# The block for outlier nodes in a four-layer graph network: selection values in two half tiles, stores one by one, loads moved ahead, clears on GpSimd

## The chip, the cores and the metric

The kernel runs on one core of one Trainium2 chip. The metric is the device time of one execution in microseconds; the kernel before takes 5758.06 us (median of three runs, 5743.28 to 5765.65). The engines are named as in the profile: PE (TensorE, with PEld for its weight loads), DVE (VectorE), ACT (ScalarE), POOL (GpSimd) and SP (SyncE, which only issues DMAs).

## The reference, cut to what matters

Sixteen graphs of 1024 nodes with 64 features pass through four layers. Before each layer the features are normalised and cut at zero. Layer 0 is the costly one. Each node drops a part of its neighbours by a rule on their rank, and then, for each of 64 features, takes the quartiles over the features of the neighbours that are left:

```python
rank = jnp.cumsum(ni, axis=-1) - ni
rem = neigh & (sk > 1) & (rank % sk == sk - 1) & mask[:, :, None]
...
s = jnp.sort(vals, axis=2)
...
for tau, w in zip(TAUS, WTS):
    pos = tau * jnp.maximum(nv - 1, 0)
    lo, hi = jnp.floor(pos), jnp.ceil(pos)
    agg = agg + w * (v_lo + frac * (v_hi - v_lo))
```

A two-matrix perceptron on x + agg follows. Layer 1 sends messages through the dense adjacency matrix into a gated recurrent unit, layer 2 sends them into a tanh layer, layer 3 is an attention over the whole matrix (a softmax over 1024 x 1024 scores). Each layer adds its result to x.

## The kernel before, in words

**The idea of layer 0.** The kernel sorts each feature over all nodes of a graph once. A quartile of a node's neighbours is then a search: for how many of the first k sorted values is the node a neighbour? These counts are matrix products of the reduced adjacency matrix with 0/1 blocks (`wt`), made for 56 words of eleven sorted values each. Signs of the counts choose the word, bit operations (`places`) choose the place in it, and matrix products with tables of value differences give candidates, from which `pick` takes one by five masked copies.

**Pairs of graphs.** The graphs go in eight pairs. For each pair there are three stages.

1. *Selection* (`weights`, `select`), one graph after the other: PE counts (L1120), ACT takes the counts out of PSUM (L1128) and makes the signs (L1175), DVE finds the word (L1186 to L1197) and picks values (L1228). It searches only the windows of words in which nearly all quartiles lie. After each graph, `compact` (L1247) gathers the few nodes, up to 64 per graph, with a quartile outside these windows: a 0/1 matrix `sel` tells which node goes to which of the 64 places, their adjacency rows come by an indirect DMA, and PE counts for all 56 words (L1311, seven pieces of 56 matmuls together). ACT copies each piece into `xr` (L1315), a buffer for two pieces; SP stores it to `x_d` in DRAM (L1316); the transposed `sel` goes to `sel_d` (L1323).
2. *The extra block* (`extras`, L1326) treats the compacted nodes of both graphs, 64 of each, as one tile of 128. ACT's queue loads the words (L1331). DVE clears two tables (L1335), and SP fills them from `t_d` in eight loads of 96-byte runs (L1337). DVE makes the biases `qx` (L1343). For three quartiles ACT shifts the words (`y_x`, two buffers, L1349), PE transposes them (L1356), ACT makes signs (L1359), and DVE takes the maxima (L1363 to L1370, with `maxima`, L1024). After `places`, there is one round for each of six statistics: PE fills the candidates `cand`, one tile of four PSUM banks (L1380), DVE picks from it (L1088) and adds to `agg_x` (L1095, L1097). Last, two rounds bring the result back to the nodes: SP loads the selection matrix into `sel_t`, one buffer (L1388), PE multiplies (L1391), DVE writes flagged nodes (L1392).
3. *Layers 0 to 3* (`layers`, L1398) of the two graphs, each with pools of its own. The first loads are `h0` (L1492) and `xb` (L1495), in two parts each; the first operation is the sum at L1497, the last the one at L1609. The blocks of the transposed adjacency matrix come from `a_d` (L1478, three buffers per graph, 48 loads a pair), in the last pair from a copy held in SBUF.

**What lies beside it.** In the stretch of stages 2 and 3, the program also prepares the next pair: `neighbours` (L883, both graphs: loads of the adjacency matrix L896, running sums on DVE L902, transposes through PE and ACT to `a_d`, the thinning rule on ACT L931 to L933) and the second half of `sort_pair`, called un-sort here (L819 to L837), which runs the sorting network backwards over codes with masks from DRAM, in groups of up to four steps. Its result goes to `y_d` (L871 to L879) and comes back as `node` (L989), from which `weights` builds the `wt` blocks (L993, L998). The first half, the sort itself (L789 to L805), lies beside the next selection. In the last pair there is no next one to prepare.

**What sets the order.** The language's scheduler gives each engine a fixed list of instructions, built from the dependences, the program's order and the places of tiles in memory. An engine works its list in order, and one that waits holds up all behind it; SP's list of DMAs too. DMAs issued from SP and ACT take eight semaphores in turn, and one waits until the last with its semaphore has landed. `tc.issue_after(x)` places what its block issues behind x in that ordering. SBUF is reused: a tile placed where an earlier one lay waits for the last use of that.

Of the kernel before, what the change touches and what calls it, by code (L numbers as in the profile page):

```python
# [9 lines left out]
F32 = mybir.dt.float32  # L10
# [13 lines left out]
P = 128  # L24
# [18 lines left out]
def gnn_stack(ctx, tc, x, adj, nodemask, w, out):  # L43
# [22 lines left out]
    nc.vector.tensor_copy(ident_b, ident)  # L66
    offdiag = const.tile([P, P], BF16, name="offdiag")
    nc.vector.tensor_scalar(offdiag, ident, -1.0, 1.0, op0=ALU.mult, op1=ALU.add)
    ones_b = const.tile([P, N], BF16, name="ones_b")
# [385 lines left out]
    def general(gw):  # L455
# [47 lines left out]
        with tc.For_i(0, B, 1) as b:  # L503
            with ExitStack() as per_batch:
# [13 lines left out]
                with (  # L518
# [3 lines left out]
                ):  # L522
                    kept = nb1.tile([P, NT, N], BF16, name="kept")
                    notrem = nb1.tile([P, NT, N], BF16, name="notrem")
                    for t in range(NT):
                        a = nb2.tile([P, N], F32, name="a", bufs=3)
                        nc.sync.dma_start(a, adj[ds(b, 1), t * P : (t + 1) * P, :].rearrange("o p j -> (o p) j"))
# [9 lines left out]
                        nc.vector.tensor_tensor_scan(cum, ones_b, ni, 0.0, op0=ALU.mult, op1=ALU.add)  # L537
# [545 lines left out]
    def pick(cand, masks):  # L1083

        v = cand.rearrange("p q (d l) -> p q d l", l=24)
        for (dst, frm, n), mk in zip(PICKS, masks):
            mk = mk.rearrange("p (q d o) -> p q d o", d=4, o=1)
            nc.vector.copy_predicated(  # L1088
                v[:, :, :, dst : dst + n], mk.to_broadcast([P, NQ, 4, n]), v[:, :, :, frm : frm + n]
            )  # L1090
        return v[:, :, :, 11]

# [157 lines left out]
    def compact(b, i, wt, row10, out_of, kept, cp, cpp):  # L1250
# [21 lines left out]
        nc.tensor.matmul(pp, ones_b[:, :P], fb[:, 1, :], start=False, stop=True)  # L1272
# [16 lines left out]
        who = cp.tile([P, 1], mybir.dt.uint32, name="who")  # L1289
        nc.vector.tensor_copy(who, pv[:, 9:10])  # L1290
        nc.scalar.copy(vx[mine, :], pv[mine, :9])
        rows = cp.tile([P, N], F8, name="rows")
        nc.gpsimd.indirect_dma_start(
            rows.bitcast(U8), None, n_d[b % 4].bitcast(U8), bass.IndirectOffsetOnAxis(ap=who, axis=0)
# [2 lines left out]
        for j0 in range(0, NT, 4):  # L1297
# [3 lines left out]
                    px[:, j, :], rows[:, (j0 + j) * P : (j0 + j + 1) * P], ident_b, start=(j == 0), stop=(j == 3)  # L1301
                )
            nc.scalar.copy(ndx[:, j0 : j0 + 4, :], px, saturate=False)
        for u in range(0, len(PIECES), 2):
            two = PIECES[u : u + 2]
            n = len(two) * 512
            xr = cp.tile([P, 1024], F32, name="xr")
            for e, g in enumerate(two):
                pw = bank()
                for j in range(NT):  # L1310
                    nc.tensor.matmul(  # L1311
                        pw, ndx[:, j, :], wt[g][:, j].rearrange("p w c -> p (w c)"),
                        start=(j == 0), stop=(j == NT - 1),
                    )
                nc.scalar.copy(xr[mine, e * 512 : (e + 1) * 512], pw[mine])  # L1315
            nc.sync.dma_start(x_d[mine, two[0] * 512 : two[0] * 512 + n], xr[mine, :n])  # L1316
        sel_t = cp.tile([P, NT, P], F32, name="sel")
        for t0 in range(0, NT, 4):
            ps = bank().rearrange("p (t n) -> p t n", n=P)
# [5 lines left out]
    def extras(pr, kept, aggs, xs, xp):  # L1325

        vx = kept["vx"]
        comb = xs.tile([P, NW * C], F32, name="comb_x")
        for u in range(0, len(PIECES), 2):
            at = slice(PIECES[u] * 512, (PIECES[u] + len(PIECES[u : u + 2])) * 512)  # L1330
            nc.scalar.dma_start(comb[:, at], x_d[:, at])  # L1331
        tabs = []
        for i in range(2):
            tab = xs.tile([4 * NH, NQ, 4, 48], F16, name=f"tab{i}")
            nc.vector.memset(tab, 0.0)  # L1335
            for d in range(4):
                taken = nc.sync.dma_start(  # L1337
                    tab[d : 4 * NH : 4, :, d, :],
                    t_d[(pr * 2 + i) * C : (pr * 2 + i + 1) * C, :NH].rearrange("(q d) h e -> d h q e", d=4)[d],
                )  # L1340
            tabs.append(tab)
        qx = xs.tile([P, 3], F32, name="qx")
        nc.vector.tensor_scalar(qx, vx[:, :3], -2048.0, -2048.0, op0=ALU.mult, op1=ALU.add)  # L1343
        signs = []
        z = xs.tile([P, 1, 6, C], U16, name="z_x")
        odd = xs.tile([P, 1, 6, C], U16, name="odd_x")
        for k in range(3):
            y = xs.tile([P, 2, 2 * NQ, 4 * NH], I16, name="y_x", bufs=2)
            nc.scalar.activation(  # L1349
                y[:, 0].rearrange("p r (h d) -> p r h d", d=4),  # L1350
                comb.rearrange("p (h r d) -> p r h d", r=2 * NQ, d=4),
                AF.Identity, bias=qx[:, k : k + 1], scale=1.0,
            )
# [12 lines left out]
            ev, od = yu[:, :, :NQ, :4], yu[:, :, NQ:, :4]  # L1366
            zs = z[:, 0, 2 * k : 2 * k + 2, :].rearrange("p s (q d) -> p s q d", d=4)
            os_ = odd[:, 0, 2 * k : 2 * k + 2, :].rearrange("p s (q d) -> p s q d", d=4)
            nc.vector.tensor_tensor(zs, ev, od, op=ALU.max)
            nc.vector.tensor_tensor(os_, od, ev, op=ALU.is_gt)  # L1370
        marks = places(xs, z, 6 * C, 1)
        aggx = xs.tile([P, C], F32, name="agg_x")
        ag = aggx.rearrange("p (q d) -> p q d", d=4)
        for s in range(6):
            cand = xp.tile([P, NQ, P], F32, name="cand")
            for q in range(NQ):
                for part in range(2):
                    for i in range(2):
                        mine = slice(i * ROOM, (i + 1) * ROOM)
                        nc.tensor.matmul(  # L1380
                            cand[mine, q, :96], signs[s][:, q, mine], tabs[i][:, q, :, part * 24 : (part + 1) * 24],
                            start=(part == 0), stop=(part == 1),
                        )
            v = pick(cand[:, :, :96], [mk[:, 0, s, :] for mk in (odd, *marks)])
            add_to(ag, s == 0, v, vx[:, 3 + s : 4 + s])
        for i in range(2):
            sel_t = xs.tile([P, NT, P], F32, name="sel_t")
            nc.sync.dma_start(sel_t, sel_d[i])  # L1388
            ps = xp.tile([P, 2, 512], F32, name="tr")[:, 0, :].rearrange("p (t c) -> p t c", c=C)
            for t in range(NT):  # L1390
                nc.tensor.matmul(ps[:, t, :], sel_t[:, t, :], aggx, start=True, stop=True)  # L1391
            nc.vector.copy_predicated(  # L1392
                aggs[i], kept["flag"][i].rearrange("p (t o) -> p t o", o=1).to_broadcast([P, NT, C]), ps
            )
        return taken.ins if hasattr(taken, "ins") else taken


    def layers(b, side_, agg, ly, lb, held=None):  # L1398

# [4 lines left out]
        def nd(name, bufs=1):  # L1404
            return ly.tile([P, NT, C], F32, name=name, bufs=bufs)

        def big():
            return nd("nd", 4)

        def packed(name, bufs=1):  # L1410
            return ly.tile([P, HALF], F32, name=name, bufs=bufs)
# [75 lines left out]
                )  # L1487


        h0 = big()  # L1490
        for f in range(2):
            nc.sync.dma_start(own(h0)[:, :, f, :], by_half(h_d[b])[:, :, f, :])  # L1492
        xb = big()
        for f in range(2):
            nc.sync.dma_start(own(xb)[:, :, f, :], by_half(x[b].rearrange("(t p) c -> p t c", p=P))[:, :, f, :])  # L1495
# [149 lines left out]
    for pr in range(pairs):  # L1645
# [2 lines left out]
        kept = {  # L1648
            "flag": [keep.tile([P, NT], U16, name=f"flag{i}") for i in range(2)],
            "vx": keep.tile([P, 9], F32, name="vx"),  # L1650
        }
        with tc.tile_pool(reuse_waits="tile", name="kn", bufs=1) as kn:
            with (
# [9 lines left out]
        with ExitStack() as beside:  # L1663
# [14 lines left out]
            with (  # L1678
# [5 lines left out]
            ):  # L1684
                if not final:
                    sop = besides.enter_context(tc.tile_pool(reuse_waits="tile", name="sop", bufs=1, space=PSUM))
                for i, (ly, lb) in enumerate(((ly0, lb0), (ly1, lb1))):
                    layers(pr * 2 + i, (pr * 2 + i) % 4, aggs[i], ly, lb, held[i])
                if pr + 1 < pairs:
                    made = prepare(pr + 1, nb, nbp)  # L1690
                    sort_pair(pr + 1, cur, sop)
# [49 lines left out]
```

## Time and profile before

| | us |
|---|---|
| median of three runs | 5758.06 |
| the profiled execution | 5775.25 |
| its span | 5773.4 |
| one pair, from words' load to words' load (fourth pair, 2779.7 to 3474.8) | 695.1 |
| extra block in it, first L1363 to first L1497 | 98.8 |
| extra block of the last pair, the same | 70.8 |

| engine | busy, us | share of the span |
|---|---|---|
| PE | 4354.5 | 75% |
| PEld | 2724.9 | 47% |
| DVE | 4997.9 | 87% |
| ACT | 3813.2 | 66% |
| POOL | 166.5 | 3% |

Three kinds of views are used below. A group line names the source line, engine, operation, output <- input and shape, then the count, the busy time in us, the mean ns of one, and the idle time of the engine just before with what ended most of it. The view by stretches gives each engine's busy time between two moments. The chain of waits goes back from the last instruction, at each step to what released it. All times are from the start of the span; a granted clock (PEclk) of 1.00 is TensorE's full speed, and the mean over the span is 0.852.

### The profile page before, as it was taken

How to read it: one execution, taken by the hardware profiler on the slowest of the kernel's cores; microseconds unless marked ns; L12 is line 12 of the kernel's file. 1: busy time of each engine (PE TensorE's matmuls, PEld its weight loads, DVE VectorE, ACT ScalarE, POOL GpSimd, SP SyncE). 2: the span in 40 equal slices, each digit the busy share in tenths (PEclk: the TensorE clock that was granted, in tenths of full speed). 3: DMA queues.
4: the chain of work that ended last, by engine and by line, in shares of the span. 5: the costliest groups of instructions: out<-in, count | busy, mean ns of one | idle time of the engine just before them, and what ended most of it. 6: DMA issues, size and time to landing. Idle time of an engine off the chain costs nothing.

```text
span 5773.4 us, 114332 instructions
## 1 busy us (share of the span) xinstructions
PE 4354.5 (75%) x45010; PEld 2724.9 (47%) x45010; DVE 4997.9 (87%) x13239; ACT 3813.2 (66%) x5763; POOL 166.5 (3%) x292
## 2 busy tenths in 40 slices
PE   1488677886778957788588885788767886779956
PEld 1355443554435544455434554355543554435642
DVE  9899888998889987999879988799888998878754
ACT  2587657775586855868568666687667866477835
POOL 3000000000000000000000000000000000000000
PEclk9699878997789978899779996899868997789967
DMA  4401264013731047210561115611255013630030
GB/s 129 127 27 41 88 208 134 26 37 107 227 96 35 28 133 232 68 37 23 158 225 53 41 45 175 199 38 40 82 173 173 28 40 90 212 113 18 10 101 5
DMA packets 519813, 551.45 MB, mean 96 GB/s; under 512 B 263297, under 2 KB 413057, under 8 KB 519265
## 3 DMA queue, kind: packets, MB, share of 16 engines
q1 hardware_dynamic: 376864, 459.65, 25.5%
q10 hardware_dynamic: 140064, 81.84, 4.6%
q8 instruction: 355, 5.82, 0.4%
q0 software_dynamic: 2336, 2.57, 0.2%
q14 instruction: 194, 1.58, 0.1%
HBM read 360.17 MB, written 183.76 MB: 94 GB/s over the span
## 4 chain that ended last, share of the span: by engine, by line
PE 34%; DVE 32%; ACT 19%; DMA 10%; issue 4%; POOL 0%; SPq 0%; ACTq 0%; DVEq 0%; POOLq 0%
PE comb L1120 11%; ACT sign L1175 6%; DVE y L1191 5%; PE cand L1220 5%; PE comb L1311 3%; PE bank L1485 3%; DVE cand L1228 3%; DMA a_d<-at 2%; ACT y L1128 2%; DVE cum L902 2%; DMA adjT<-a_d 2%; DVE s L793 1%; DVE s L792 1%; PE pk L952 1%; DVE swapped L791 1%
## 5 line engine op out<-in xcount | busy, mean ns | idle before, releaser
L1120 PE MATMUL comb<-wt,ndT 128*128 128x512 fp8e5 x6144 | 1435.6, 385 | 136.3 <-ACT sign L1175 112.1
L1128 ACT ACTIVATE y<-comb,qb 128x512 int16<-128x512 f32 x1152 | 743.5, 711 | 497.2 <-PE comb L1120 497.2
L1120 PEld LDWEIGHTS <-ndT 128*128 128x128 fp8e5 x6144 | 589.3, 98 | 852.9 <-issue 222.2
L1175 ACT ACTIVATE sign<-comb,lower 128x1024 fp8e5<-128x1024 int16 (+1 forms) x640 | 694.1, 1085 | 0.0
L1175 ACT ACTIVATE sign<-comb,half 128x1024 fp8e5<-128x1024 int16 (+1 forms) x640 | 688.9, 1076 | 0.0
L1220 PE MATMUL cand<-vtab,sign 128*128 128x48 f16 (+1 forms) x18432 | 668.4, 191 | 25.1 <-DVE agg L1097 15.2
L1220 PEld LDWEIGHTS <-sign 128*128 128x128 fp8e5 x18432 | 641.7, 96 | 85.1 <-issue 23.9
L1191 DVE TENSOR_TENSOR y<-y 128x512 uint16<-128x512 uint16 (+5 forms) x896 | 670.1, 790 | 10.5 <-PE comb L1173 10.0
L1228 DVE COPY_PREDICATED cand<-w_f,cand 128x256 f32<-128x256 uint16 (+1 forms) x1536 | 532.7, 378 | 84.1 <-PE cand L1220 81.7
L1173 PE MATMUL comb<-ident_b,y 128*128 128x128 bf16 x4608 | 307.0, 218 | 102.2 <-ACT sign L1175 70.2
L910 ACT COPY at<-pk 128x512 f32<-128x512 f32 x256 | 147.2, 585 | 351.6 <-PE pk L908 177.2
L952 PE MATMUL pk<-minus_b,rem 128*128 128x128 bf16 x1024 | 231.4, 251 | 175.6 <-ACT rem L933 175.6
L1173 PEld LDWEIGHTS <-y 128*128 128x128 bf16 x4608 | 284.8, 97 | 127.2 <-issue 127.1
L952 PE MATMUL pk<-ident_b,ni 128*128 128x128 bf16 x1024 | 227.0, 247 | 108.0 <-ACT ndT L958 63.4
L902 DVE TENSOR_TENSOR_SCAN cum<-ni 128x1024 f16<-128x1024 fp8e5 x128 | 292.3, 2284 | 17.7 <-POOL ni L898 14.4
L1485 PE MATMUL bank<-att,hs 128*64 128x512 f32 x512 | 195.7, 876 | 143.5 <-ACT hs L1601 143.5
L908 PE MATMUL pk<-ident,a 128*128 128x128 f32 x1024 | 188.0, 330 | 144.8 <-DMA a<-in_adj_dram 92.0
L998 DVE TENSOR_SCALAR wt<-node 128x2048 uint8<-128x2048 f16 x224 | 263.3, 1219 | 21.9 <-PE comb L1311 21.9
L1485 PE MATMUL bank<-adjT,nd 128*64 128x512 f32 x896 | 255.5, 638 | 29.7 <-DMA adjT<-a_d 29.2
L792 DVE TENSOR_TENSOR s<-s 128x384 f32<-128x384 f32 (+4 forms) x440 | 263.2, 598 | 0.0
L793 DVE TENSOR_TENSOR s<-s 128x384 f32<-128x384 f32 (+4 forms) x440 | 262.1, 596 | 0.0
L1186 DVE TENSOR_SCALAR y<-y 128x4608 int16<-128x4608 int16 x128 | 173.6, 1356 | 97.6 <-ACT y L1128 96.7
(382 smaller groups left out, 8340.5 us busy)
## 6 DMA issues: line engine op xcount, KB each, us to landing
adjT<-a_d SPq DMA_DIRECT2D x336, 512.0 KB
a<-in_adj_dram SPq DMA_DIRECT2D x128, 512.0 KB
a_d<-at ACTq DMA_DIRECT2D x256, 256.0 KB
m_d<-swapped SPq DMA_DIRECT2D x104, 512.0 KB
swapped<-m_d SPq DMA_DIRECT2D x104, 512.0 KB
n_d<-nat SPq DMA_DIRECT2D x128, 128.0 KB
x_d<-xr SPq DMA_DIRECT2D x48, 256.0 KB
comb_x<-x_d ACTq DMA_DIRECT2D x24, 512.0 KB
```

Source lines behind the costliest of these rows:

```text
L792: nc.vector.tensor_tensor(to_lo, lo, hi, op=ALU.max)
L793: nc.vector.tensor_tensor(to_hi, lo, hi, op=ALU.min)
L902: nc.vector.tensor_tensor_scan(cum[:, t - t0, :], ni[:, t, :], wide[:, t, pad - 1 : pad - 1 + N], 0.0, op0=ALU.add, op1=ALU.add)
L952: nc.tensor.matmul(pk[:, n % 4, :], lhs, rhs, start=(n % 4 == 0 and m == 0), stop=(m == len(terms) - 1 and last),)
L1120: nc.tensor.matmul(pw, ndT[:, j, t * P : (t + 1) * P], wt[1 + g8][:, j].rearrange("p w c -> p (w c)"), start=(j == 0), stop=(j == NT - 1),)
L1128: nc.scalar.activation(y[:, 0, chunks, at : at + 8 * d_].rearrange("p q (w d) -> p q w d", d=d_), pw.rearrange("p (w q d) -> p q w d", w=8 ...
L1173: nc.tensor.transpose(pt[:, q - q0, :], y[:, 0, q, :].bitcast(BF16), ident_b)
L1175: nc.scalar.activation(signs[tl][s][:, q0:q1, :], pt.bitcast(I16), AF.Sign, bias=before[s], scale=-1.0, saturate=False,)
L1191: nc.vector.tensor_tensor(v[:, :, :, :n], v[:, :, :, :n], v[:, :, :, n : 2 * n], op=ALU.max)
L1220: nc.tensor.matmul(cand[:, e, at : at + 12 * d_].rearrange("p (d l) -> p d l", l=12), signs[tl][sec][:, chunk, :], tab[:, q, :, half_ * 12 ...
L1228: nc.vector.copy_predicated(v[:, :, :, dst : dst + k], mk.to_broadcast([P, 2, C // 2, k]), v[:, :, :, frm : frm + k])
L1485: nc.tensor.matmul(po[to : to + C, :], lhs, rhs[:, f * HALF : (f + 1) * HALF], start=(j == 0), stop=(j == NT - 1))
```

## The change

Six things are changed in and around the extra block.

- `compact`: each of seven pieces has its own buffer of 512 words (three buffers) and its own store, where two pieces shared one buffer and one store. The bias `qx` is made here, for the 64 rows of each graph, and kept.
- `extras`: the tables are cleared by POOL instead of DVE, and SP's table loads are put behind the last load of words.
- The two selection matrices are loaded together before `places`, into the buffers that `y_x` used, where each was loaded before its own matmuls. The two results lie in the two banks of one PSUM tile.
- The candidates of a statistic are made and picked in two halves, with two tiles of two banks each, where there was one tile of four.
- `loads` is new: it issues `h0` and `xb` of both graphs ahead of the layers, into tiles of the first graph's pool.
- The constant of ones shrinks from 1024 to 128 columns; the general path makes its own.

The diff, cut to its core:

```diff
+        nc.vector.tensor_scalar(kept["qx"][mine], pv[mine, :3], -2048.0, -2048.0, op0=ALU.mult, op1=ALU.add)
...
-        for u in range(0, len(PIECES), 2):
-            two = PIECES[u : u + 2]
-            n = len(two) * 512
-            xr = cp.tile([P, 1024], F32, name="xr")
-            for e, g in enumerate(two):
-                pw = bank()
...
-                nc.scalar.copy(xr[mine, e * 512 : (e + 1) * 512], pw[mine])
-            nc.sync.dma_start(x_d[mine, two[0] * 512 : two[0] * 512 + n], xr[mine, :n])
+        for g in PIECES:
+            xr = cp.tile([P, 512], F32, name="xr", bufs=3)
+            pw = bank()
...
+            nc.scalar.copy(xr[mine], pw[mine])
+            nc.sync.dma_start(x_d[mine, g * 512 : (g + 1) * 512], xr[mine])
...
-            nc.scalar.dma_start(comb[:, at], x_d[:, at])
-            nc.vector.memset(tab, 0.0)
-            for d in range(4):
-                taken = nc.sync.dma_start(
+            loaded = nc.scalar.dma_start(comb[:, at], x_d[:, at])
+        tabs = [xs.tile([4 * NH, NQ, 4, 48], F16, name=f"tab{i}") for i in range(2)]
+        for tab in tabs:
+            nc.gpsimd.memset(tab, 0.0)
+        with tc.issue_after(loaded.ins if hasattr(loaded, "ins") else loaded):
+            for i, tab in enumerate(tabs):
+                for d in range(4):
+                    taken = nc.sync.dma_start(
...
-        qx = xs.tile([P, 3], F32, name="qx")
-        nc.vector.tensor_scalar(qx, vx[:, :3], -2048.0, -2048.0, op0=ALU.mult, op1=ALU.add)
+        qx = kept["qx"]
...
+        sel_t = xs.tile([P, 2, 2 * NQ, 4 * NH], I16, name="y_x", bufs=2)
+        sel_t = sel_t.rearrange("p e r h -> p (e r h)").bitcast(F32)[:, : 2 * N].rearrange("p (i t n) -> p i t n", i=2, n=P)
+        for i in range(2):
+            nc.sync.dma_start(sel_t[:, i], sel_d[i])
         marks = places(xs, z, 6 * C, 1)
...
         for s in range(6):
-            cand = xp.tile([P, NQ, P], F32, name="cand")
-            for q in range(NQ):
+            for q0 in range(0, NQ, NQ // 2):
+                at = slice(q0 * 4, q0 * 4 + C // 2)
+                cand = xp.tile([P, NQ // 2, P], F32, name="cand", bufs=2)
+                for q in range(q0, q0 + NQ // 2):
...
-            v = pick(cand[:, :, :96], [mk[:, 0, s, :] for mk in (odd, *marks)])
-            add_to(ag, s == 0, v, vx[:, 3 + s : 4 + s])
+                v = pick(cand[:, :, :96], [mk[:, 0, s, at] for mk in (odd, *marks)])
+                add_to(ag[:, q0 : q0 + NQ // 2], s == 0, v, vx[:, 3 + s : 4 + s])
+        both_ = xp.tile([P, 2, 512], F32, name="tr")
         for i in range(2):
-            sel_t = xs.tile([P, NT, P], F32, name="sel_t")
-            nc.sync.dma_start(sel_t, sel_d[i])
...
+    def loads(b, ly):
+        two = []
+        for src in (h_d[b], x[b].rearrange("(t p) c -> p t c", p=P)):
+            to = ly.tile([P, NT, C], F32, name=f"nd{b % 2}", bufs=4)
+            for f in range(2):
+                nc.sync.dma_start(
+                    to.rearrange("p (t f) c -> p t f c", f=2)[:, :, f, :],
+                    src.rearrange("p (f t) c -> p t f c", f=2)[:, :, f, :],
+                )
+            two.append(to)
+        return two
...
+                heads = [loads(pr * 2 + i, ly0) for i in range(2)]
                 for i, (ly, lb) in enumerate(((ly0, lb0), (ly1, lb1))):
-                    layers(pr * 2 + i, (pr * 2 + i) % 4, aggs[i], ly, lb, held[i])
+                    layers(pr * 2 + i, (pr * 2 + i) % 4, aggs[i], ly0, ly, lb, *heads[i], held[i])
```

More of the change, by code (lines that the diff above doesn't have):

```diff
@@ L68, in gnn_stack @@
     nc.vector.tensor_scalar(offdiag, ident, -1.0, 1.0, op0=ALU.mult, op1=ALU.add)
-    ones_b = const.tile([P, N], BF16, name="ones_b")
+    ones_b = const.tile([P, P], BF16, name="ones_b")
     nc.vector.memset(ones_b, 1.0)
@@ L524, in general @@
                     notrem = nb1.tile([P, NT, N], BF16, name="notrem")
+                    ones_n = nb1.tile([P, N], BF16, name="ones_n")
+                    nc.vector.memset(ones_n, 1.0)
                     for t in range(NT):
@@ L536, in general @@
                         cum = nb2.tile([P, N], F32, name="cum")
-                        nc.vector.tensor_tensor_scan(cum, ones_b, ni, 0.0, op0=ALU.mult, op1=ALU.add)
+                        nc.vector.tensor_tensor_scan(cum, ones_n, ni, 0.0, op0=ALU.mult, op1=ALU.add)
                         nbi = nb2.tile([P, 1], I32, name="nbi")
@@ L1088, in pick @@
             nc.vector.copy_predicated(
[L1089 removed]
+                v[:, :, :, dst : dst + n], mk.to_broadcast([P, mk.shape[1], 4, n]), v[:, :, :, frm : frm + n]
             )
@@ L1271, in compact @@
         nc.tensor.matmul(pp, below, fb[:, 0, :], start=True, stop=False)
-        nc.tensor.matmul(pp, ones_b[:, :P], fb[:, 1, :], start=False, stop=True)
+        nc.tensor.matmul(pp, ones_b, fb[:, 1, :], start=False, stop=True)
         over = cp.tile([P, 1], F32, name="over")
@@ L1303, in compact @@
             nc.scalar.copy(ndx[:, j0 : j0 + 4, :], px, saturate=False)
-        for u in range(0, len(PIECES), 2):
-            two = PIECES[u : u + 2]
-            n = len(two) * 512
-            xr = cp.tile([P, 1024], F32, name="xr")
-            for e, g in enumerate(two):
-                pw = bank()
[L1310 to L1315, printed above, removed]
-            nc.sync.dma_start(x_d[mine, two[0] * 512 : two[0] * 512 + n], xr[mine, :n])
+        for g in PIECES:
+            xr = cp.tile([P, 512], F32, name="xr", bufs=3)
+            pw = bank()
+            for j in range(NT):
+                nc.tensor.matmul(
+                    pw, ndx[:, j, :], wt[g][:, j].rearrange("p w c -> p (w c)"),
+                    start=(j == 0), stop=(j == NT - 1),
+                )
+            nc.scalar.copy(xr[mine], pw[mine])
+            nc.sync.dma_start(x_d[mine, g * 512 : (g + 1) * 512], xr[mine])
         sel_t = cp.tile([P, NT, P], F32, name="sel")
@@ L1330, in extras @@
             at = slice(PIECES[u] * 512, (PIECES[u] + len(PIECES[u : u + 2])) * 512)
-            nc.scalar.dma_start(comb[:, at], x_d[:, at])
[L1332 to L1335, printed above, removed]
-            for d in range(4):
-                taken = nc.sync.dma_start(
[L1338 to L1341, printed above, removed]
-        qx = xs.tile([P, 3], F32, name="qx")
-        nc.vector.tensor_scalar(qx, vx[:, :3], -2048.0, -2048.0, op0=ALU.mult, op1=ALU.add)
+            loaded = nc.scalar.dma_start(comb[:, at], x_d[:, at])
[6 more added lines that the diff above has]
+                    taken = nc.sync.dma_start(
+                        tab[d : 4 * NH : 4, :, d, :],
+                        t_d[(pr * 2 + i) * C : (pr * 2 + i + 1) * C, :NH].rearrange("(q d) h e -> d h q e", d=4)[d],
+                    )
+        qx = kept["qx"]
         signs = []
@@ L1374, in extras @@
         for s in range(6):
-            cand = xp.tile([P, NQ, P], F32, name="cand")
-            for q in range(NQ):
[L1377 to L1383, printed above, removed]
-            v = pick(cand[:, :, :96], [mk[:, 0, s, :] for mk in (odd, *marks)])
-            add_to(ag, s == 0, v, vx[:, 3 + s : 4 + s])
+            for q0 in range(0, NQ, NQ // 2):
+                at = slice(q0 * 4, q0 * 4 + C // 2)
+                cand = xp.tile([P, NQ // 2, P], F32, name="cand", bufs=2)
+                for q in range(q0, q0 + NQ // 2):
+                    for part in range(2):
+                        for i in range(2):
+                            mine = slice(i * ROOM, (i + 1) * ROOM)
+                            nc.tensor.matmul(
+                                cand[mine, q - q0, :96], signs[s][:, q, mine], tabs[i][:, q, :, part * 24 : (part + 1) * 24],
+                                start=(part == 0), stop=(part == 1),
+                            )
+                v = pick(cand[:, :, :96], [mk[:, 0, s, at] for mk in (odd, *marks)])
+                add_to(ag[:, q0 : q0 + NQ // 2], s == 0, v, vx[:, 3 + s : 4 + s])
+        both_ = xp.tile([P, 2, 512], F32, name="tr")
         for i in range(2):
-            sel_t = xs.tile([P, NT, P], F32, name="sel_t")
-            nc.sync.dma_start(sel_t, sel_d[i])
-            ps = xp.tile([P, 2, 512], F32, name="tr")[:, 0, :].rearrange("p (t c) -> p t c", c=C)
+            ps = both_[:, i, :].rearrange("p (t c) -> p t c", c=C)
             for t in range(NT):
-                nc.tensor.matmul(ps[:, t, :], sel_t[:, t, :], aggx, start=True, stop=True)
+                nc.tensor.matmul(ps[:, t, :], sel_t[:, i, t, :], aggx, start=True, stop=True)
             nc.vector.copy_predicated(
@@ L1395, in extras, with layers @@
         return taken.ins if hasattr(taken, "ins") else taken
-    def layers(b, side_, agg, ly, lb, held=None):
+    def loads(b, ly):
[6 more added lines that the diff above has]
+                    src.rearrange("p (f t) c -> p t f c", f=2)[:, :, f, :],
+                )
+            two.append(to)
+        return two
+    def layers(b, side_, agg, front, ly, lb, h0, xb, held=None):
         H2 = NT // 2
@@ L1407, in big @@
         def big():
-            return nd("nd", 4)
+            return front.tile([P, NT, C], F32, name=f"nd{b % 2}", bufs=4)
         def packed(name, bufs=1):
@@ L1487, in gather @@
                 )
[L1490 to L1495, printed above, removed]
         o0 = big()
@@ L1650, in gnn_stack @@
             "vx": keep.tile([P, 9], F32, name="vx"),
+            "qx": keep.tile([P, 3], F32, name="qx"),
         }
```

## The prediction, made before the changed kernel was run

> **What bounds the kernel now.** The page first: VectorE (DVE) is busy 87% of the span (4997.9 us), and none of the 40 slices falls under 7 tenths before the last two. PE and DVE share the chain of work that ended last.
>
> ```profile
> span 5773.4 us, 114332 instructions
> ...
> DVE  9899888998889987999879988799888998878754
> ...
> PE 34%; DVE 32%; ACT 19%; DMA 10%; issue 4%; POOL 0%; SPq 0%; ACTq 0%; DVEq 0%; POOLq 0%
> ```
>
> A mean of 87% says little, so next the view by stretches: for the fourth pair (they repeat to a few us) from the loads of the extra block's words to its first VectorE operation, to the first layer operation, to the first matmul of the next selection, to the next pair's words; then the block and the layers of the last pair.
>
> ```profile
> core 0: us, PE busy (x) PEld busy (x) DVE busy (x) ACT busy (x) POOL busy (x), PEclk, DMA share, GB/s
> 2779.70:2793.90 14.20, 0.00 (x0) 0.00 (x1) 8.75 (x17) 3.33 (x2) 1.79 (x4) 0.50 0.79 225
> 2793.90:2892.70 98.80, 57.70 (x792) 49.96 (x792) 93.52 (x223) 66.06 (x87) 6.18 (x10) 0.66 0.49 144
> 2892.70:3070.40 177.70, 139.56 (x704) 65.42 (x705) 141.39 (x452) 120.89 (x165) 3.68 (x7) 0.79 0.58 194
> 3070.40:3474.80 404.40, 345.50 (x4131) 223.63 (x4129) 376.46 (x961) 286.67 (x469) 4.30 (x9) 0.95 0.16 47
> 5536.30:5607.10 70.80, 30.00 (x464) 28.06 (x464) 41.05 (x91) 17.82 (x9) 0.32 (x2) 0.50 0.39 129
> 5607.10:5766.60 159.50, 112.59 (x407) 50.83 (x407) 81.68 (x269) 79.05 (x107) 2.88 (x4) 0.72 0.01 2
> ```
>
> In the first seven pairs the block takes 98.8 us and VectorE is busy 93.5 of them: the next pair's sort and neighbour work fills its waits, so only 5.3 us are there to be won. In the last pair nothing fills it: 70.8 us with 41 busy. There each statistic of the block runs matmuls, then picks, in turn, as the chain in time shows (start, us, what):
>
> ```profile
> 5572.83 2.79 PE cand L1380 x64
> 5575.64 0.97 DVE cand L1088
> 5576.64 0.44 DVE cand L1088
> 5577.10 0.44 DVE cand L1088
> 5577.56 0.31 DVE cand L1088
> 5578.50 2.79 PE cand L1380 x64
> ```
>
> One round is 5.67 us, of which 2.8 are VectorE's. VectorE's groups in the last block (busy, mean ns | idle before, releaser):
>
> ```profile
> L1088 DVE COPY_PREDICATED cand<-odd_x,cand 128x768 f32<-128x768 uint16 x6 | 5.8, 961 | 14.5 <-PE cand L1380 14.5
> L1088 DVE COPY_PREDICATED cand<-w_f,cand 128x256 f32<-128x256 uint16 x12 | 5.1, 427 | 0.3
> ...
> L1335 DVE MEMSET tab<- 112x1536 uint32 x2 | 2.7, 1338 | 0.5 <-issue 0.5
> ...
> L1392 DVE COPY_PREDICATED agg<-flag,tr 128x512 f32<-128x512 uint16 x2 | 1.4, 723 | 10.2 <-PE tr L1391 10.2
> ```
>
> **The last pair, part by part.** *Halves.* By the tile view a pick of 768 elements takes 955 ns and one of 256 takes 422: 1.04 ns an element and 155 ns each. One statistic is now 955+422+422+278+222+278 = 2577 ns. A half is 384, 128, 128, 64, 32 and an add of 32: 555+278+278+222+189+245 = 1767, two of them 3534; +957 ns. In the changed program's order the picks of the halves lie among each other, and three of the second half's (0.8 us) stand behind the last of the first. Its refill by PE takes half of 2.79, and some 0.15 for the signal, so 0.75 us stay open. Round: 3.6+0.75 = 4.35 for 5.67, five rounds: -6.6; the first statistic lies behind the masks and costs +0.9. *Matrices and inputs early.* Now the second matrix is asked for at 5599.4, after the first's matmuls, and h and x behind it on SP until 5604.5; the first layer operation starts at 5607.1. With all in place the first graph can start after its matmuls and copy (5595.7+3.7+0.7 = 5600.1), the second at 5604: 7 and 4 us earlier, on two chains that share the engines; I take -5. *Words one by one.* ACT waits for the store of its only buffer before the next copy:
>
> ```profile
> ACT xr L1315 <- DMA x_d<-xr: 133.9, 48, 4.5
> ```
>
> That is 2.8 us each. The last store leaves at 5520.3 though its matmuls end at 5516.5; with three buffers it leaves at 5517.2. The last load of words is issued behind that store (5524.6) and landed at 5532.2; the clears with qx behind them ended at 5533.0, so the early qx alone is worth 0.8. Together -3.9; I take -3.5, since the adjacency loads on the same DMA engines stay. Three more stores per graph, at 0.45 us of SP each, stand ahead of nothing that is late. *Clears by GpSimd.* Not in the trace at this size; the nearest row is its clear of 128x2048 uint16 in 1802 ns, VectorE's own 1338: between 1.3 and 2.7 us each, I take 2.7 (by elements). Tables may come 3 us later; the first masked pick needs them some 20 us later. Without that cover it would be up to +2.7. GpSimd's neighbour products queue behind the clears; VectorE's scans (L902) wait for these. Sum for the last pair: -6.6+0.9-5-3.5 = **-14.2 us**.
>
> [...]
>
> [...]
>
> **The seven other pairs.** The order of instructions of the changed program differs far more than the diff: the next pair's work moves. I add up the mean durations of the rows of before along VectorE's order, from the block's first operation (durations overlap a little, so these are units, not us):
>
> - To the first layer operation: before 107.9, after 83.1, picks of +5.7 included. Before took 98.8 us with 5.3 idle; at the same rate 83.1 x 93.5/107.9 + 5.3 = 77.3 us. So the layers start 21.5 us earlier, but only because filling work is put later.
> - The layers, first operation to last (second L1609): before 176.6 units in 185 us, 37.7 of them idle; after 170.9. Alone, in the last pair, they take 159.5 us. By units 179, by the unchanged chain 185; I take 182 (bounds 160 and 195).
> - What is put off: before, the un-sort (L824 to L837) ends at 219.3 units, 30 before the layers do, and its result's way over DRAM lay hidden. After, it ends at 271.2, alone, 16.5 after the layers. The next weights (L993) need it: L871 1.05, transposes and casts 2.3, two stores 1.3 and 2.7 to land, the load 0.6 and 2.5: 10.4 us, under which the next sort's norm (7 units) lies. So 26.5 us from the layers' end to L993 (bounds 18 and 33).
> - L993 then comes 77.3+182+26.5 = 285.8 us after the block's first operation, before 273.0: +12.8.
> - From there to the next block: 471.7 units before, 467.4 after: -4.3 x 0.89 = -4. And ACT's wait for stores falls in the middle of the selection: VectorE's gap before L998 there is 2.9, I take -2 (bounds 0 and -5). The 2.7 us of clears bring nothing: VectorE idles 4.9 us right behind them, for y_x.
>
> Sum: +12.8-4-2 = **+6.8 a pair, +47.6 in seven.** On SP the matrix loads now wait for a y_x buffer that VectorE's second maxima free, some 10 us in; behind them stand masks of the un-sort, which VectorE frees later still, and adjacency loads that before were issued only at 2832, so I cost that at nothing. Further on, eight loads of h and x and six of adjT pass a mask load, and the next masks stand behind 28 adjT loads.
>
> All: +47.6-14.2 = +33 us. The profiled execution took 5775.25 (span 5773.4, 1.9 around it); the median of the runs is 5758.06, 17 less. I set the sum on the median: 5758+33 = **5791**.
>
> **Rivals.** *Faster: the early start is kept.* The layers have their h, x and six adjT blocks in place and fewer fills among them; if they run in 168 us, near the 159.5 alone, a pair gains 7.2, in all -50-14 = -64: 5694. It decides below 177 us, where the pairs' loss equals the last pair's gain. For it: in the chain of this stretch adjT loads and a_d stores end several waits. Against: each fill that is moved out comes after. *Within 0.5%: both cancel.* Layers 178, way of the codes 25: +1.3 a pair, 5753. Here belongs the case that the early loads are not early: the table loads' order is tied to a load on ACT's queue, but SP itself waits only for the clears. *Slower still: the un-sort starves.* If the masks behind adjT loads (each freed by a gather) come late, VectorE has no fill in the second pass; 11 us more in the layers give +17.8 a pair: 5868.
>
> **How the numbers follow.** Forecast 0.32, faster rival 0.27, cancelling 0.27, starving 0.14. One half per cent is about what a measurement here can tell. Faster 0.27, within 0.27, slower 0.32+0.14 = 0.46. The range takes in most of the outer rivals' spread: 5690 to 5868.
>
> **What would show it.** Per pair: first layer operation some 77 us after the first L1363, second L1609 at 259, L993 at 286; in the last pair rounds of 4.3 us and the block some 10 us shorter. Wrong would be a layer stretch under 177 us, or an un-sort that ends well before the layers.

## The result, and the profile after

The changed kernel takes 5813.32 us (median of six runs, 5801.22 to 5826.89), the kernel before in the same comparison 5757.75 (six runs, 5743.28 to 5774.27): a ratio of 1.0094, 95% interval 1.0076 to 1.0112. It is slower by 55.6 us; the forecast was +33.

The page of the changed kernel (span, VectorE's 40 slices, shares of the chain that ended last):

```profile
span 5809.6 us, 114773 instructions
...
DVE  9999878998799987998889988899888998887765
...
DVE 37%; PE 32%; ACT 16%; DMA 11%; issue 3%; POOL 0%; SPq 0%; ACTq 0%; DVEq 0%; POOLq 0%
```

VectorE is as full as before, and its share of the chain has grown from 32% to 37%. The view by stretches, for the fourth pair from the block's first VectorE operation to the first layer operation, to the layers' end, to the first weights (L995, L993 before), to the next pair's block; then the block and the layers of the last pair (columns as in the table of before):

```profile
2813.10:2887.50 74.40, 42.33 (x608) 36.77 (x608) 69.41 (x193) 53.34 (x62) 1.15 (x4) 0.66 0.42 124
2887.50:3065.40 177.90, 138.09 (x726) 65.39 (x727) 147.15 (x423) 118.07 (x167) 9.32 (x13) 0.84 0.65 212
3065.40:3093.00 27.60, 11.93 (x169) 9.94 (x166) 19.24 (x80) 12.66 (x19) 0.00 (x0) 0.69 0.33 73
3093.00:3517.40 424.40, 346.88 (x4127) 224.08 (x4127) 388.64 (x990) 291.94 (x473) 18.65 (x13) 0.92 0.17 52
5585.00:5645.30 60.30, 28.91 (x464) 26.95 (x464) 43.57 (x127) 17.63 (x8) 0.38 (x2) 0.56 0.44 156
5645.30:5803.50 158.20, 110.92 (x407) 50.56 (x407) 81.62 (x269) 79.18 (x107) 2.78 (x4) 0.73 0.01 2
```

The block is 24 us shorter than before and the layers 8 us. But a third stretch is new. Between the layers' end and the first weights lie 27.6 us, of which VectorE works 19.2 and PE 11.9; before, the first weights came ahead of the layers' end. The chain of waits through the end of this stretch (start, us, what) shows the way of the codes:

```profile
3082.01 0.64 DVE code L839
3082.64 0.02 issue
3082.67 1.07 ACT s L873
...
3086.72 0.59 ACT s L879
3087.32 0.02 issue
3087.33 2.92 DMA y_d<-s
3090.25 0.02 issue
3090.27 2.67 DMA node<-y_d
3092.93 0.02 issue
3092.96 0.07 DVE node L995
```

From the end of the last un-sort operation (3082.65) to the codes' landing (2.67 us after 3090.27) it takes 10.3 us, in the open, as forecast.

In the last pair the rounds of the chain are these:

```profile
5622.91 2.79 PE cand L1385 x64
5625.70 0.02 issue
5625.73 1.22 DVE cand L1090 x5
5626.95 0.15 DVE agg_x L1099
5627.10 0.15 DVE cand L1090
5627.25 2.79 PE cand L1385 x64
```

One round is 4.34 us, for 5.67 before. PE still stands whole on the chain with 2.79 us; the halves take half of VectorE's part off it.

Where the difference lies, from the traces of both kernels and of those that follow. Means over the seven filled pairs, counted from the block's first operation; "period" is block to block, "gather" is GpSimd's gather of the first graph's rows (below):

| kernel | block | layers | un-sort ends | first weights | from there on | period | gather |
|---|---|---|---|---|---|---|---|
| before | 99.5 | 185.5 | 219.8 | 271.8 | 419.7 | 691.5 | 1.0 |
| changed | 75.5 | 177.7 | 269.1 | 279.4 | 419.7 | 699.1 | 6.5 |
| halves_only | 82.3 | 187.4 | 275.2 | 285.4 | 413.6 | 699.1 | 1.0 |
| halves_last | 95.0 | 186.7 | 244.1 | 275.0 | 421.1 | 696.1 | 6.5 |
| halves_last_bias | 94.7 | 185.6 | 242.1 | 273.4 | 417.1 | 690.6 | 1.0 |
| bias_late | 76.6 | 174.9 | 267.1 | 277.4 | 415.5 | 692.9 | 1.0 |
| matrices_late | 80.0 | 180.0 | 257.7 | 270.2 | 419.2 | 689.3 | 6.5 |
| loads_late | 76.8 | 178.8 | 263.7 | 273.9 | 421.7 | 695.6 | 6.5 |
| after_direct | 77.5 | 178.0 | 271.7 | 277.0 | 424.5 | 701.5 | 6.5 |
| unsort_ahead | 77.3 | 190.9 | 241.7 | 293.4 | 411.4 | 704.8 | 1.0 |
| last_only | 100.1 | 185.5 | 220.0 | 272.2 | 418.0 | 690.2 | 1.0 |

By the two profiled executions the sum is -4.6 us up to the first block, +53.2 in seven pairs, -12.4 in the last: +36.2. The medians differ by 55.6. Most of the gap is the trace of before, which was 17 us above its median. `last_only` (below) has the same instruction order in the filled pairs, and it reaches the last block 14.9 us earlier (5521.4 for 5536.3).

Work and waits can be told apart by VectorE's busy time on the first line of each page; the rest of the span it is idle:

| kernel | span | VectorE busy | idle |
|---|---|---|---|
| before | 5773.4 | 4997.9 | 775.5 |
| last_only | 5748.7 | 4996.4 | 752.3 |
| halves_last_bias | 5754.0 | 5002.4 | 751.6 |
| halves_last | 5790.0 | 5001.4 | 788.6 |
| before_dup | 5807.6 | 5038.0 | 769.6 |
| changed | 5809.6 | 5034.4 | 775.2 |
| bias_late | 5769.0 | 5037.2 | 731.8 |
| matrices_late | 5749.3 | 5023.3 | 726.0 |
| unsort_ahead | 5858.9 | 5036.0 | 822.9 |

With the added picks in the filled pairs VectorE is busy 5023 to 5041 us in every kernel of this document, without them 4996 to 5002. The idle time goes from 726 to 823 us with the order and the gather. Before and last_only, with the same order in the filled pairs, differ by 23 us of idle time; some 10 of these are the last pair's shorter block, and the rest shows how far single executions of one order lie apart.

### The profile page after: what moved, and what is told of

It is laid out like the page before. It is cut to its first block, busy times and chain, and to the rows that moved or that the text cites. A ratio compares the mean times of both kernels' runs of the same rounds, so it can differ in the third digit from the quotient of the medians.

```text
span 5809.6 us, 114773 instructions
## 1 busy us (share of the span) xinstructions
PE 4320.3 (74%) x45010; PEld 2712.1 (47%) x45010; DVE 5034.4 (87%) x13519; ACT 3811.5 (66%) x5753; POOL 257.3 (4%) x308
## 4 chain that ended last, share of the span: by engine, by line
DVE 37%; PE 32%; ACT 16%; DMA 11%; issue 3%; POOL 0%; SPq 0%; ACTq 0%; DVEq 0%; POOLq 0%
PE comb L1122 10%; ACT sign L1177 5%; DVE y L1193 5%; PE cand L1222 4%; PE comb L1311 4%; DVE cand L1230 3%; PE bank L1502 3%; DMA a<-in_adj_dram 2%; DVE cum L904 2%; ACT y L1130 2%; DMA adjT<-a_d 2%; DVE wt L1000 2%; DMA a_d<-at 2%; PE pk L954 2%; DVE code L839 2%
## 5 line engine op out<-in xcount | busy, mean ns | idle before, releaser
L1000 DVE TENSOR_SCALAR wt<-node 128x2048 uint8<-128x2048 f16 x224 | 261.6, 1219 | 53.1 <-PE comb L1311 52.6
```

The costliest lines, as they stand in the source:

```text
L1000: nc.vector.tensor_scalar(wt[g][:, :, k : k + 4, :].bitcast(U8), node, 4.0 * (25 + CODE * (8 * g + k)), 4.0 * 26, op0=ALU.add, op1=ALU.min,)
```

## The experiments

Ratios are to the kernel before on the same chip, with 95% intervals. "Order" is the theory on which the prediction rests: the un-sort is put behind the layers, and the way of its codes lies open. "Work" is its rival: the added picks cost their time on a full VectorE, wherever they lie. The busy times above show that both hold in part: the picks cost some 35 us of busy time (21 to 45) in every order, and the order decides over the idle time.

**Halves in the last pair only** (`halves_last`).

```diff
+        half = NQ // 2 if pr + 1 == B // 2 else NQ
         for s in range(6):
-            for q0 in range(0, NQ, NQ // 2):
+            for q0 in range(0, NQ, half):
...
-                cand = xp.tile([P, NQ // 2, P], F32, name="cand", bufs=2)
+                cand = xp.tile([P, half, P], F32, name="cand", bufs=NQ // half)
```

> All of the change, but the candidates are made in two halves only in the last pair; in the seven filled pairs they lie in one tile as before. In VectorE's order the un-sort then ends 27 us of work ahead of the layers' end (in the changed kernel 14 behind it). Theory 'order' (the halves push the un-sort behind the layers, where its tail and the way of the codes over DRAM lie open): the 7.6 us of idle time ahead of the first weights go, and the 5.7 us of picks with them, so 8 to 13 us a pair less than the changed kernel: some 5735 us (5722 to 5757). Rival 'work' (only the 36 more pick instructions cost, idle time just moves): 5813 - 7 x 5.7 = 5773. Rival 'other parts' (clears, stores, early loads cost, not the halves): 5813, no change.

Measured: 5795.27 us, 1.0054 (1.0035 to 1.0073). All three missed. The un-sort ends in time and the open wait is gone, yet a pair takes 696.1 us, 4.6 more than before. Something else costs as well, and VectorE's waits show where: it waits for PE's words (L1311) ahead of a weight block, 53.7 us here, 52.6 in the changed kernel, 21.9 before:

```profile
DVE wt L998 <- PE comb L1311: 21.9, 7, 3.8
```

**Halves alone** (`halves_only`): the kernel before with only the loop over halves of the change and its shorter constant of ones.

```diff
-            cand = xp.tile([P, NQ, P], F32, name="cand")
...
+            for q0 in range(0, NQ, NQ // 2):
...
+                cand = xp.tile([P, NQ // 2, P], F32, name="cand", bufs=2)
```

> The kernel before with the halves in all pairs and nothing else of the change (the constant of ones is shortened too, as there). In VectorE's order the un-sort ends 4 us of work behind the layers. 'Order': a filled pair costs 6 to 9 us more than before, as in the changed kernel, and the last gains 6: 5758 + 52 - 6, some 5803 (5790 to 5820). 'Work': 5758 + 7 x 5.7 - 6 = 5792. 'Other parts': 5752, at or under the kernel before.

Measured: 5818.94, 1.0096 (1.0069 to 1.0123): at the upper end of the range of "order", 27 us above "work". The halves alone make the new order, with the un-sort 5.5 us behind the layers, and cost as much as the whole change. The wait for words is not in this one (its gather takes 1.0 us): halves and other parts do not add up. The last pair's block is 63.9 us for 70.8: the halves gain 6.9 there.

**The codes of the first graph kept in SBUF** (`after_direct`); for room, the words' stores have two buffers here instead of three.

```diff
             nc.scalar.copy(cn[:, q : q + 4, :], pc)
+            nc.scalar.copy(code_y[:, q : q + 4, :], pc[:, :, :C])
...
-        nc.sync.dma_start(node[:, :, 0, :], y_d[b])
+        if b % 2:
+            nc.sync.dma_start(node[:, :, 0, :], y_d[b])
+        else:
+            nc.scalar.copy(node[:, :, 0, :], code_y)
```

> The changed kernel, but the codes of each pair's first graph do not go over DRAM: ACT copies them from PSUM into a tile that stays, and the weights are built from that (the words' stores have two buffers instead of three, for room). 'Order': the 5.0 us that VectorE stands before the first weights for the load of the codes go, 5 us a pair: 5813 - 35 = 5778, and the idle time between the layers' end and the first weights falls from 7.6 to about 2.6. 'Work': the wait comes back elsewhere in the selection, 5813 within 10.

Measured: 5821.3, 1.0101 (1.0081 to 1.0121): no gain. The number is the one of "work" (5813 within 10), but the run does not tell the theories apart. DRAM is out of the first graph's way, but VectorE's wait is still there, now for ACT's copies, 42.0 us in all:

```profile
DVE node L999 <- ACT code_y L881: 42.0, 8, 5.3
```

The next sort's norm, which lay under the codes' way, stands behind the first weights here, so nothing covers what is left of the way. The first weights come 4.7 us sooner after the layers (21.5 for 26.2), and the stretch behind them is 4.8 us longer.

**Picks done twice** (`before_dup`): in the kernel before, both picks of 256 elements again, in the filled pairs.

```diff
+            if again and n == 4:
+                nc.vector.copy_predicated(
+                    v[:, :, :, dst : dst + n], mk.to_broadcast([P, NQ, 4, n]), v[:, :, :, frm : frm + n]
+                )
```

> The kernel before, with the two picks of 256 elements of each statistic done twice in the seven filled pairs: 12 more instructions of 422 ns, 5.1 us of VectorE a pair, and no halves. VectorE's order keeps the un-sort 36 us of work ahead of the layers' end. 'Work': the full price, 7 x 5.1 = 36: 5794. 'Order' alone: VectorE idles 38 us a pair in the layers, where fills can make room, so a part of the price only: 5758 to 5780.

Measured: 5801.71, 1.0068 (1.0046 to 1.009): +39 us (26 to 52 by the interval) for 36 us of work. Work in the block is paid in full within this interval, as "work" says: VectorE is busy 40 us longer and idles 6 us less. The un-sort ends later here too (250.6 us for 219.8), so the order did not stay as it was.

**Clears alone, and clears undone** (`clears_only`, `clears_back`): in the kernel before by GpSimd (with the shorter constant of ones), in the changed kernel by VectorE.

```diff
-            nc.vector.memset(tab, 0.0)
+            nc.gpsimd.memset(tab, 0.0)
```

> The kernel before with the tables cleared by GpSimd, and nothing else of the change but the shorter constant. In the traces of the changed kernel and of the one with halves in the last pair only, GpSimd's gather of the first graph's rows in compact takes 6.5 us in pairs two to eight (1.0 us in the kernel before and with the halves alone), and VectorE's wait for the words' matmuls ahead of a weight block grows from 19 to 50 us in seven pairs. Theory 'gather' (the clears cause the slow gather, and it costs 31 us): the gather takes 6.5 us here too, and with 8 x 2.7 us of clears off VectorE the time is 5763 - 21 + 31 = 5773. Rival 'gather is slow for another reason' (the early bias or the stores one by one): the gather takes 1.0 us and the time is 5742 or up to no change.

> The changed kernel with the tables cleared by VectorE again. 'Gather': it takes 1.0 us again, the wait for the words' matmuls falls back to 19 us, and 5813 - 31 + 21 = 5803. Rival: clears on VectorE are plain work and the gather stays slow: 5834.

Measured: 5755.09, 0.999 (0.9978 to 1.0002), and 5851.35, 1.0162 (1.0146 to 1.0178). The theory that GpSimd's clears slow its gather fell: it takes 1.0 us in the first and 6.5 in the second. In the kernel before, clears on GpSimd are worth 6 us, at most 13; in the changed kernel 39, though VectorE's 16 clears come to some 21 us. `clears_back` is 17 us above the rival's 5834 too. The order changed again (the first weights come at 285.4 us of the pair), which may be the rest; no run shows it.

**The next sort ahead** (`unsort_ahead`).

```diff
-                    sort_pair(pr + 1, cur, sop)
+                    with tc.high_priority(offset=800):
+                        sort_pair(pr + 1, cur, sop)
```

> The changed kernel, with the next pair's sort and un-sort given to the scheduler 800 places earlier, so that in VectorE's order the un-sort ends 22 us of work ahead of the layers' end (14 behind it in the changed kernel) and the way of the codes over DRAM lies under the layers again. Some 18 us of other next-pair work comes behind the layers instead. 'Order': the 7.6 us of idle time between the layers and the first weights go, -5 to -8 us a pair: 5813 - 35 to - 53, some 5770. Rival 'work' (VectorE's list has the same work, and idle time that goes here comes back elsewhere): 5813 within 12.

Measured: 5852.65, 1.0155 (1.0139 to 1.0172), a clear miss. The un-sort ends 26.5 us before the layers do, and the wait for codes is gone. But what was in its place is late now: the next sort waits for its own input,

```profile
DVE swapped L793 <- ACT s L777: 59.4, 6, 10.4
```

and the first weights come 14 us later. An un-sort in time is not enough: here another part of the next pair's preparation came late in its place. The gather is quick in this kernel (1.0 us), so the loss is not the gather's.

**The whole change, in the last pair only** (`last_only`): every part bound to the last pair as the halves are above, except that the table loads are not put behind the loads of words in any pair.

> All parts of the change in the last pair only (halves, stores one by one, early bias, early matrices, early h and x, clears by GpSimd); the seven filled pairs keep the lists of the kernel before. The last pair's gain alone: 5763 - 14 = 5749 (5740 to 5756), under both kernels. If it is not under 5757, a gain seen in the last pair's stretch is paid elsewhere.

Measured: 5740.26, 0.9963 (0.9945 to 0.998): 21 us faster than the kernel before and some 75 faster than the changed one. Its last block takes 61.1 us (70.8 before).

**The bias late** (`bias_late`, and `halves_last_bias` with halves in the last pair only).

```diff
-        nc.vector.tensor_scalar(kept["qx"][mine], pv[mine, :3], -2048.0, -2048.0, op0=ALU.mult, op1=ALU.add)
...
-        qx = kept["qx"]
+        qx = xs.tile([P, 3], F32, name="qx")
+        nc.vector.tensor_scalar(qx, vx[:, :3], -2048.0, -2048.0, op0=ALU.mult, op1=ALU.add)
```

> The changed kernel with the bias qx made in the extra block again, as before; VectorE's order is the same but for some 180 of 12509 places. In all traces with the slow gather (6.5 us for 1.0) VectorE does the early bias just ahead of it, and the wait of GpSimd ends with the bias; the traces without it have another instruction there. 'Gather by the bias': it takes 1.0 us again, VectorE's wait for the words' matmuls falls from 50 to some 19 us in seven pairs, and the time is 5813 - 31 = 5782. Rival 'the gather is not on the path': 1.0 us too, but the wait comes back elsewhere: 5813 within 12. If it stays at 6.5, the bias is not the cause.

> All of the change with halves in the last pair only, and the bias made in the extra block as before. The kernel with the early bias took 5795. 'Gather by the bias': 5795 - 31 = 5764, about the kernel before; then nothing but the gather stands against the last pair's gain. Rival 'not on the path': 5795 within 12.

Measured: 5774.74, 1.0041 (1.0025 to 1.0057), and 5755.45, 1.0003 (0.9986 to 1.002). Both as the theory has it: 31 and 29 us less than with the early bias. GpSimd's gather in the changed kernel (count, then ns: least, median, most), and what ended GpSimd's waits ahead of it:

```profile
L1296 POOL DMA_INDIRECT rows<-n_d,who x16: 952/1026/6518, 446.2 to 5549.1; - x16
its engine sat idle before it (us, times) until:
  DVE qx L1294: 1473.3, 6
```

and with the bias late:

```profile
L1295 POOL DMA_INDIRECT rows<-n_d,who x16: 951/1000/1322, 443.5 to 5504.8; - x16
its engine sat idle before it (us, times) until:
  DVE swapped L793: 1470.8, 6
```

Six gathers, in pairs two to seven, start as the bias ends, and take six times as long as the others. The rows are late for PE (its weight loads wait for them 102.7 us in all, with the bias late 74.9), PE's words are late, and VectorE stands ahead of a weight block. In the changed kernel, and with the bias late (21.9 us before, above):

```profile
DVE wt L1000 <- PE comb L1311: 52.6, 7, 8.5
```

```profile
DVE wt L1000 <- PE comb L1310: 24.3, 8, 4.1
```

**Loads late, matrices late** (`loads_late`, `matrices_late`): the changed kernel with `h0` and `xb` loaded inside `layers`, and with each selection matrix loaded before its matmuls, as before.

```diff
-                heads = [loads(pr * 2 + i, ly0) for i in range(2)]
```

```diff
-        for i in range(2):
-            nc.sync.dma_start(sel_t[:, i], sel_d[i])
...
         for i in range(2):
+            sel_t = xs.tile([P, NT, P], F32, name="sel_t")
+            nc.sync.dma_start(sel_t, sel_d[i])
```

> The changed kernel without the early loads of h and x. In the last pair, where no order is at stake, the block's end to the first layer operation is longer by what the early loads are worth: of the 5 us forecast for matrices and inputs together, 1 to 4. In the filled pairs VectorE's order has the un-sort's end 8 us of work behind the layers instead of 14. If the early loads make the layers quicker (177.7 us for 185.5 before), they take 182 to 187 here and the time is 5813 + 7 x 4 = 5841; if the order does that, they stay under 180 and the time at 5813 within 15.

> The changed kernel with each selection matrix loaded before its own matmuls again. Last pair: the two rounds at the end wait for a load each, block longer by 3 to 5 us. Filled pairs: in VectorE's order the un-sort ends with the layers (0.7 us of work ahead; 14 behind in the changed kernel). 'Order': L993's wait for the codes shrinks, -3 to -6 us a pair: 5813 - 30 = 5783. 'Work': 5813 + 5.

Measured: 5774.5, 1.0035 (1.0015 to 1.0054), and 5739.78, 0.9976 (0.9958 to 0.9994). For the first neither expectation fits: the layers stay quick (178.8), so the loads are not what makes them so, and yet 34 us go; which part of the order brings them is open. In the second the last pair's block is 63.7 us, for 60.3 in the changed kernel and 61.1 to 61.3 in the other kernels with early matrices, so the early matrices gain 2.6 to 3.4 there; without them the filled pairs gain 9.8 us each, twice what "order" expected. VectorE's waits for the gates of layer 1, for the adjacency loads and for the codes in the kernel before,

```profile
DVE rn L1542 <- ACT att L1540: 19.3, 8, 11.5
DVE ni L897 <- DMA a<-in_adj_dram: 16.6, 14, 2.4
DVE node L993 <- DMA node<-y_d: 1.8, 3, 0.9
```

in the changed kernel,

```profile
DVE rn L1553 <- ACT att L1551: 80.5, 45, 11.5
DVE ni L899 <- DMA a<-in_adj_dram: 44.1, 33, 3.8
DVE node L995 <- DMA node<-y_d: 41.2, 9, 10.3
```

and with the matrices late:

```profile
DVE rn L1550 <- ACT att L1548: 50.1, 27, 11.5
DVE ni L899 <- DMA a<-in_adj_dram: 22.6, 23, 2.2
DVE node L995 <- DMA node<-y_d: 6.7, 3, 5.3
```

The un-sort ends 11.4 us earlier in the pair and ahead of the layers' end (257.7 of 260.0), the neighbours' last running sum 38 us earlier (172.8 for 210.8), and the open wait for codes goes: 34.5 of the 68 us. The early matrices do not hold SP up: in the changed kernel's fourth pair the mask load behind them is issued 0.1 us after them, at 2830.4. What is left as their cost is the order that they bring about. The matrices and the bias both late, the two gains together, were not tried.

## Why the prediction was right, and where not

**The sum.** Four of these kernels make a ladder, each rung one more part: everything in the last pair only, 0.9963; the other parts in the filled pairs too, with the bias late, 1.0003; halves there as well, 1.0041; the early bias, 1.0094. In us: -21, +23, +22, +31, together +55; each step is known to some 14 us. By the single profiled executions they are -25, +5, +15 and +41, so the second is the least certain. The forecast had the first three kinds (-14 for the last pair; the new order and the picks) and not the fourth. That its sum a pair (+6.8) met the measured +7.6 is partly luck: it had 5.2 us too much up to the first weights and 6 us too little behind them.

- *Block, forecast 77.3 us from 98.8*: 74.4 in the fourth pair. Right.
- *Layers 182*: 177.9. The size is off by 4, towards the faster rival, which was to decide below 177 us; the mean is 177.7, and its condition was just missed.
- *Way from the layers' end to the first weights 26.5*: 27.6 in the fourth pair, 26.2 in the mean, the open route 10.3 us for 10.4. Right. The wait in it (41.2 us in all) is shown by the two traces; what it costs is not shown by itself. In `matrices_late` 34.5 us of it go together with other waits and 68 us of time. In `halves_last_bias` it goes too (1.1 us, for 40.6 in `bias_late`), yet VectorE idles 20 us more there, and the layers are longer (185.6 us for 174.9). No kernel moved the un-sort and nothing else.
- *First weights at 285.8 us of the fourth pair, 12.8 later*: at 279.9, and 7.6 later in the mean; 2.9 of the 5.9 us between are the block's, 4.1 the layers', less 1.1 of the way. The 273.0 us of before, from which the 12.8 were counted, is where the first `wt` block (L998, 3066.92) starts; L993 itself starts at 269.7 (3063.62). So the forecast's own times are 16.1 us apart, and the measured ones of the fourth pair 10.2.
- *From there to the next block -4 -2*: 0.0. This is the step that failed. ACT's wait for stores did go (133.9 us before, none after), but "I take -2" of VectorE's gap before L998 became +4.4 a pair (52.6 less 21.9, over seven): the gather came late in its place. The prediction priced the early bias in the last pair alone (0.8 us), and did not ask what its instruction stands ahead of in the other seven: `bias_late` gives 31 us. With the bias late this stretch is 415.5 us, 4.2 less than before: that fits the -4 of the moved work, and the -2 does not show.
- *Picks at 155 ns + 1.04 ns an element*: 561 and 222 ns for the forecast 555 and 222 (384 and 64 elements). In busy time they are paid nearly in full in every order (some 35 us, for 40 forecast); in the time of the kernel the halves of the filled pairs are a cost of 22 us on the ladder and of some 62 alone (`halves_only`, its last pair's gain set aside).
- *Last pair -14.2*: rounds 4.34 us for 4.35; block -10.5 for -10.7. Halves 6.9 for 5.7; matrices 2.6 to 3.4 and loads up to 1 for 5 together. From PE's last words to the block 17.3 us for 19.8, and PE done 0.7 us sooner: 3.2 for 3.5. Right.
- *Clears at nothing in the filled pairs*: `clears_only` gives 0.999, with an interval that holds no change. They take 2655 ns each on GpSimd, the 2.7 us that was taken.
- *Matrix loads at nothing on SP*: right for SP, but taking the edit out gives 68 us; the forecast had its effect only inside the order as a whole, and could not have said which edit brings it.
- *Baseline*: +33 was set on the median of before while it was worked out against an execution 17 us slower. That is most of the 22 us between 5791 and 5813: the two profiled executions are only 36.2 us apart.

## What to carry to other kernels

Where one engine is full, look at its busy time and its idle time apart: here added work showed in the first whatever the order (21 to 45 us), and the second moved by more (726 to 823 us). A change to a short block is then decided by what the scheduler does with the work that filled its waits: follow the fill to its new place, and ask what it must deliver, and when. An edit worth having only where nothing fills the waits belongs only there: bound to the last pair, this change is worth 21 us, everywhere it costs 55. Of each instruction that is moved, even one of 0.15 us, ask what it stands directly ahead of.

## What the runs showed of the hardware that was not expected

GpSimd's gather (an indirect DMA) takes some 1.0 us (0.95 to 1.4) or 6.2 to 6.5 us, with nothing between. What tells them apart is the bias, an operation of 0.15 us on 64x3 elements. In the seven kernels here with the early bias in all pairs, all 36 gathers that start after its end are slow (34 of them within 0.03 us of it, two 0.31 us after), and all that start before its end are quick: the other ten of the changed kernel's 16, and all of `unsort_ahead`, where one more operation stands between the gather's release and the bias. Each slow one in the changed kernel ends 0.9 us after a gapless run of VectorE operations that goes on for 5.6 us from its start; in the two slow ones of 6.2 us the run goes on for 5.3 us, and they too end 0.9 us after it. So the end of a slow gather goes with the end of VectorE's run. The bias and the gather of the fourth pair (start, us, what) in the changed kernel,

```profile
2562.47 0.14 DVE L1294 TENSOR_SCALAR qx<-comb 64x3 f32<-64x3 f32 x1
...
2562.63 6.52 POOL L1296 DMA_INDIRECT rows<-n_d,who  x1 [244.82 <-DVE qx L1294]
```

and the gather with the bias late:

```profile
2542.62 0.29 DVE L1047 TENSOR_SCALAR w_m<-z 128x512 uint16<-128x512 uint16 x1
...
2542.78 1.02 POOL L1295 DMA_INDIRECT rows<-n_d,who  x1 [242.53 <-DVE swapped L793]
```

The slow gathers agree with a wait for the end of VectorE's run. That is the author's reading: no trace here shows what holds them, and none splits the 0.9 us into the rest of a wait and the gather's own work. But with the bias late, and in the kernel before, the same gather passes in 1.0 us while VectorE works on for 5.6 us without a gap. That the place of the bias decides is shown; why the gather gets through the same run of operations without it is open.
